# Layer 1 of a graph network on one core: one float32 product a block in place of a float16 and a float32r product

## The chip, the cores and the metric

One program runs on one core of a Trainium2 chip. The metric is the device time of one execution in microseconds (us). A core has a matrix engine (TensorE, PE in the profile; its weight loads are listed apart as PEld), a vector engine (VectorE, DVE), an activation engine (ScalarE, ACT), a general engine (GpSimd, POOL) that issues the indirect transfers, and SyncE (SP) that issues plain ones. SBUF is the on-chip memory of 128 partitions, PSUM the memory that products accumulate in.

## The reference

A layer norm and a relu, then four layers of a graph network over 6250 nodes and 100000 edges, which are sorted by their destination. What the layers compute, cut down:

```python
h = jnp.maximum(_layernorm(x, axis=-1), 0.0)                        # 6250 x 256
deg = segment_sum(ones, dst)
h = h @ W1_self + (segment_sum(h[src], dst) / clip(deg, 1)) @ W1_neigh + b1     # 256 -> 512
hp = relu(h @ W2_pool + b2_pool)
h = h @ W2_self + where(deg > 0, segment_max(hp[src], dst), 0) @ W2_neigh + b2
h = ((segment_sum(h[src], dst) + h) / (deg + 1)) @ W3_neigh + b3
h = h @ W4_self + (segment_sum(h[src], dst) / clip(deg, 1)) @ W4_neigh + b4
out = x + h @ W_fc + b_fc                                           # 6250 x 256
```

The change is in the first `segment_sum(h[src], dst)` and in the rows `h` that it sums.

## The kernel before, in words

The nodes are 49 tiles of 128 (`NT` = 49). Weight matrices that follow one another without a nonlinearity are multiplied together beforehand (`product`). The edges that end in the first tiles are many, since the destinations crowd at low numbers. So layer 1 forms its neighbour sums in two ways.

- **Dense tiles**, the first 12 (`H1`). For each of them a matrix `A` of edge counts (128 x 128 for each of the 49 source tiles, 8-bit) is built by products of one-hot matrices (`build`, `build_narrow`; tile `pb`). Then `dense` multiplies the 49 blocks of `A` with the 49 tiles of rows of `h` and accumulates in the PSUM tile `pd`: 12 x 49 = 588 blocks. A copy of `A` widened to 32 bits (`af`, made by ScalarE) is the stationary operand of the second product.
- **Gathered tiles**, the other 37. `sums` goes through 402 groups of 128 edges. For each, GpSimd gathers the 128 source rows from the table `tab_h` in HBM into a slot of `ring` (13 slots), VectorE writes a one-hot matrix `hot` of the destinations, and PE sums the rows into `pg`. After every four groups VectorE adds `pg` to the accumulators `acc` of the tiles concerned.

`sums` leads: behind each group it calls `hub.advance`, which lays a share of the waiting dense and build products behind it, and steps finished tiles (`done1`) on. A finished tile is divided by its degree, transposed, and multiplied with `Wa` and `Wb`; `turn_h0` transposes the tile's own rows. A scheduler may then move instructions within an engine. In the prologue VectorE's order is fixed by hand.

The rows of `h` are held twice: `Z1h` is the row times 2^20 rounded to float32r, `Z1l` is what the rounding left, as float16. Three more columns of `Z1l` hold 1, the tile's number and the partition's number, so that the same sums also give the degree and a node's sum of source indices. The prologue makes them in 17 groups of three tiles: `stats` and `inverse` (VectorE) find mean and deviation, `scaled` (ScalarE) writes the relu of the normalised row over `xt` and a scaled copy into `Z1h`, `lower` (VectorE) subtracts to get `Z1l` and stores both parts into `tab_h` (386 words a row). Beside this, the prologue sorts out the edges: `row_begins` multiplies one-hot matrices `sel` (float32) with starts `SN` (4 blocks with one product each and 4 blocks with four, 20 in all, into `pa`), and the builds of the first dense tile begin.

So each block takes two products into the same PSUM tile, first the float16 one with 256 + 3 columns, then the float32r one with 256. In `dense`:

```python
nc.tensor.matmul(hold[0][:, : F + extra], a[1], z[1][:, : F + extra], ...)   # L601: float16, 8-bit A
nc.tensor.matmul(hold[0][:, :F], a[0], z[0], ...)                            # L606: float32r, af
```

and in `sums` the same on lines 545 and 548. Products in plain float32 also occur: the weight products (L285), `done1`'s with `Wa` (L1197) and `Wb` (L1203; two for each of 49 tiles), and `row_begins`' (L855). Transposes through PE are products with an identity (`ident`); the ones of `done1`'s means are on L1185.

Layers 2 to 4 follow with tables of their own, and have their own dense and gathered parts that use `sums` and `dense` in other forms.

Of the kernel before, what the change touches and what calls it, by code (L numbers as in the profile page):

```python
# [21 lines left out]
P = 128  # L22
# [7 lines left out]
WIN, WIN2 = 8, 4  # L30
HUB = (12, 23, 23)
WIDE_BUILT = 8
UP = float(2 ** 20)
UP3 = float(2 ** 12)
ROOM3, SEEN3 = float(2 ** 28), float(2 ** 11)
EARLY = (8, 40)
# [52 lines left out]
def fast_path(  # L89
# [81 lines left out]
    const = ctx.enter_context(tc.tile_pool(name="fconst", bufs=1))  # L171
    dram = ctx.enter_context(tc.tile_pool(name="fdram", bufs=1, space=DRAM))

    tab_h = dram.tile([NP, FI + FI // 2 + 2], F32, name="tab_h")
    tab_t = dram.tile([NT, P, FH], F32, name="tab_t")
    tab_r = dram.tile([NP, FH + FH // 2], F32, name="tab_r")
    tab_s = dram.tile([NP, 2 * FO], F32, name="tab_s")
# [323 lines left out]
        return tc.issue_after(ins[0].ins) if ins else nullcontext()  # L501

    def sums(pool, psg, table, F, srcT, keyT, jb, h, done, deep, hub, wait=0, counts=0, todo=None, rest=0,
             wide=False, aside=(), open_accs=3, spare_hots=4):

        ring = pool.tile([P, deep, table.shape[1]], F32R, name="ring", bufs=1)
# [12 lines left out]
        def gather(j):  # L524
            nc.gpsimd.indirect_dma_start(  # L525
                out=ring[:, j % deep, :].bitcast(F32),
                out_offset=None, in_=table,
                in_offset=bass.IndirectOffsetOnAxis(ap=srcT[:, j - jb : j - jb + 1], axis=0),
            )

        for j in range(j0, j0 + ahead):
            one_hot(j)
        for g in range(g_of[h][0], NG):
            pg = bank(psg, "pg", "pg", (2 * F if wide else F + counts,))
            n = min(G, T - g * G)
            for k in range(n):
                j = g * G + k
                X = ring[:, j % deep, :]
                gather(j)
                if j + ahead < T:  # L540
                    one_hot(j + ahead)
                if wide:
                    nc.tensor.matmul(pg, hot[j], X, start=(k == 0), stop=(k == n - 1))  # L543
                else:
                    nc.tensor.matmul(pg[:, : F + counts], hot[j].bitcast(BF16)[:, 1::2],  # L545
                                     X.bitcast(F16)[:, 2 * F : 3 * F + counts],
                                     start=(k == 0), stop=False)
                    mm = nc.tensor.matmul(pg[:, :F], hot[j], X[:, :F], start=False,  # L548
                                          stop=(k == n - 1))
                if counts and j == T - 1:  # L550
                    ended.append(mm)
                del hot[j]
                at = j - j0 + 1
                if at > wait:
                    hub.advance(before + math.ceil((len(hub.work) - before) * (at - wait)
                                                   / (T - j0 - wait - rest)))
                while len(pair) < 2 and todo:
                    pair.append([todo.pop(0), 0])
                for i, t in enumerate(list(pair)):
                    if i and pair[0] is not t and pair[0][1] < 5:  # L560
                        break
                    t[1] += 1
                    if next(t[0], None) is None:
                        pair.remove(t)
                if aside and next(aside[0], None) is None:
                    aside.pop(0)
            for d in range(h, NT):
                g0, g1 = g_of[d]
                if not g0 <= g <= g1:
                    continue  # L570
                m = M[:, m_at[d] + g - g0 : m_at[d] + g - g0 + 1]
                for half in (pg[:, :F], pg[:, F:]) if wide else (pg,):
                    if d not in acc:
                        acc[d] = pool.tile([P, F + counts], F32, name="acc", bufs=open_accs)
                        nc.vector.tensor_scalar(acc[d], half, m, None, op0=ALU.mult)
                    else:
                        nc.vector.scalar_tensor_tensor(acc[d], half, m, acc[d],  # L577
                                                       op0=ALU.mult, op1=ALU.add)
                if g == g1:
                    todo.append(done(d, acc.pop(d)))  # L580
        while aside:
            for _ in aside.pop(0):
                pass
        for t in [t for t, _ in pair] + list(todo):
            for _ in t:
                pass
        del todo[:]

    def dense(ss, block, rows, F, psd, done, extra=0, wide=False, own=None):

        hold = {}

        def run(s):
# [3 lines left out]
            z = rows(s)  # L597
            if wide:
                nc.tensor.matmul(hold[0], a[0], z, start=(s == ss[0]), stop=(s == ss[-1]))  # L599
            else:  # L600
                nc.tensor.matmul(hold[0][:, : F + extra], a[1], z[1][:, : F + extra],  # L601
                                 start=(s == ss[0]), stop=False)
# [33 lines left out]
    def segments():  # L636
# [15 lines left out]
        for b, tb in enumerate(BLOCKS):  # L652
# [20 lines left out]
    nc.gpsimd.memset(Z1l[:, :, FI:], 1.0)  # L673
    nc.gpsimd.iota(Z1l[:, :, FI + 1], pattern=[[1, NT]], base=0, channel_multiplier=0,
                   allow_small_or_imprecise_dtypes=True)
    nc.gpsimd.iota(Z1l[:, :, FI + 2], pattern=[[0, NT]], base=0, channel_multiplier=1,
                   allow_small_or_imprecise_dtypes=True)
    w1pool = layer1.enter_context(tc.tile_pool(name="w1", bufs=1))
    Wa = w1pool.tile([P, KI, FH], F32, name="Wa")
# [18 lines left out]
    with ExitStack() as pro:  # L698
# [59 lines left out]
        def scaled(g):  # L758
# [8 lines left out]
            nc.scalar.activation(Z1h[:, i0 : i0 + LG, :], xt, AF.Copy, scale=UP)  # L767

        def lower(g):
            i0, LG = groups[g]  # L770
            rows = tab_h[i0 * P : (i0 + LG) * P, :]
            hi, lo = Z1h[:, i0 : i0 + LG, :], Z1l[:, i0 : i0 + LG, :]
            nc.vector.scalar_tensor_tensor(lo[:, :, :FI], xts[g], UP, hi.bitcast(F32),
                                           op0=ALU.mult, op1=ALU.subtract)
            nc.sync.dma_start(rows[:, :FI].rearrange("(c p) f -> p c f", p=P), hi.bitcast(F32))
            nc.sync.dma_start(rows[:, FI:].rearrange("(c p) f -> p c f", p=P), lo.bitcast(F32))


        win_of = ep.tile([P, RB * P], F16, name="win_of")
# [254 lines left out]
                rN, dflat[1 : EX + 1].rearrange("(c p e) -> p c e", p=P, e=P)))  # L1034

        def products1():
            yield from product(ep, pst, psm, W1_self, w2p, Wa, 1, 1.0 / UP)
            yield from product(ep, pst, psm, W1_neigh, w2p, Wb, 1, 1.0 / UP)
            yield from bias_rows(psm, b1c, w2p, crow, b2p)

        steps = products1()
# [83 lines left out]
    with ExitStack() as on:  # L1125
# [4 lines left out]
        wk = on.enter_context(tc.tile_pool(name="fl1", bufs=2))  # L1130

        def h0_row(s):
            return Z1h[:, s, :], Z1l[:, s, :]

        def turn_h0(pt, d):
            for k in range(KI):
                c = slice(k * P, (k + 1) * P)
                nc.tensor.matmul(pt[:, k, :], Z1h[:, d, c], ident_r, start=True, stop=False)
# [85 lines left out]
        def widened(i):  # L1224
            if i < len(pieces):
                d, s0 = pieces[i]
                wide[i] = wk.tile([P, LG, P], F32R, name="af", bufs=3)
                nc.scalar.copy(wide[i], As[d % 2][:, s0 : s0 + LG, :])

        def block1(d, s):  # L1230
# [3 lines left out]
            if s % LG == (4 if s >= NT - LG else 0):  # L1234
# [1 line left out]
            return wide[i][:, s % LG, :], As[d % 2][:, s, :]  # L1236

        denses = [dense(range(NT), lambda s, d=d: block1(d, s), h0_row, FI, psd,
                        lambda acc, d=d: todo.append(done1(d, acc)), extra=3)
                  for d in range(H1)]  # L1240
# [7 lines left out]
        sums(wk, psg, tab_h, FI, srcT, keyT, JC * P, H1, done1, 13, hub, counts=3, todo=todo, rest=24, spare_hots=3,  # L1248
             aside=[own_ahead(), tail_checks(wk), segments()])
    layer1.close()  # L1250

# [121 lines left out]
    with tc.tile_pool(name="fl2c", bufs=1) as ck, ExitStack() as late:  # L1373
# [38 lines left out]
        def products2(wp):  # L1412
# [18 lines left out]
            yield from prod(W1_self, us, usA, 1.0 / UP)  # L1431
            yield from prod(W1_neigh, us, usB, 1.0 / UP)
# [382 lines left out]

    upto2.close()

    def stream(pool, chunks, wide_pool, deep=4, ahead=2):

        got = {}  # L1820
        where = {(d, s): i for i, (d, s0, s1) in enumerate(chunks) for s in range(s0, s1)}
# [12 lines left out]
        def widened(i):  # L1834
            if i < len(chunks):
                n = chunks[i][2] - chunks[i][1]
                wide[i] = wide_pool.tile([P, most_wide, P], F32R, name="af", bufs=ahead + 2)
                nc.scalar.copy(wide[i][:, :n, :], got[i][:, :n, :])  # L1838

        for i in range(deep):  # L1840
# [783 lines left out]
```

## Time and profile before

| | |
|---|---|
| median of 3 runs | 2554.43 us (2551.59 to 2556.82) |
| profiled execution | 2551.33 us |
| its span on the core | 2549.5 us |
| mean granted TensorE clock | 0.936 |
| moved by transfers | 781.10 MB |

The profile is of one execution. Its page gives each engine's busy time, strips of 40 equal slices of the span, the transfer queues, the chain of work that ended last, and groups of instructions. A group's row reads: line, engine, operation, what it writes and reads by the program's names (out<-in), shapes, count | busy us, mean ns of one | idle time of the engine just before them and what ended it. The times of overlapping products each include the time in which a result drains, so a group's mean is more than what a product takes from the next one. In the timeline a row is start, length, engine, line and operation, with a count where equal ones are merged. A wait reads: engine, what waited <- what it waited for: us in total, times, longest.

### The profile page before, as it was taken

Reading aid. Unit: us, or ns where it says so; the run is one execution under the profiler, and the core shown is the slowest. Engines: PE = TensorE matmul, PEld = TensorE weight load, DVE = VectorE, ACT = ScalarE, POOL = GpSimd, SP = SyncE. Lnnn points to the kernel's source line nnn. Section 1 sums busy time; section 2 is a strip of 40 time slices with the busy share of each in tenths; the row PEclk is TensorE's granted clock in tenths of the full one; section 3 lists DMA queues with packets and bytes.
Section 4 is the critical chain, followed back from the end, with each engine's and each line's share of the span. In section 5 each row is a group of like instructions: output and inputs, shape, how many; then the busy total and the mean of one; then the engine's idle time right before and its main releaser. Section 6 shows DMA issues by size and latency. Waiting matters only on the chain.

```text
span 2549.5 us, 35257 instructions
## 1 busy us (share of the span) xinstructions
PE 2171.2 (85%) x9379; PEld 1259.7 (49%) x9379; DVE 2044.3 (80%) x5490; ACT 1289.6 (51%) x2685; POOL 1732.9 (68%) x2018
## 2 busy tenths in 40 slices
PE   4789999999687565679999999896399999799987
PEld 2346666767443222234444444342144444488766
DVE  7899998876599899888989999788657778377656
ACT  5679988566378887765323333231112222354443
POOL 5466776667476776777667666677477777477775
PEclk9899999999898787899999999898699999899999
DMA  9667777678799999999999999999799999899996
GB/s 313 177 191 212 215 214 216 203 218 240 248 382 321 332 362 346 335 365 357 342 319 338 343 330 304 302 358 317 255 376 401 402 406 392 292 341 342 324 308 212
DMA packets 380302, 781.10 MB, mean 306 GB/s; under 512 B 56718, under 2 KB 176118, under 8 KB 380060
## 3 DMA queue, kind: packets, MB, share of 16 engines
q0 software_dynamic: 134800, 470.32, 55.4%
q1 hardware_dynamic: 155816, 216.23, 23.5%
q10 hardware_dynamic: 89476, 92.21, 10.9%
q8 instruction: 76, 1.25, 0.2%
q14 instruction: 134, 1.10, 0.1%
HBM read 569.93 MB, written 209.41 MB: 306 GB/s over the span
## 4 chain that ended last, share of the span: by engine, by line
PE 49%; DMA 26%; DVE 13%; issue 4%; ACT 4%; POOL 3%; ACTq 0%; SPq 0%; DVEq 0%; POOLq 0%
PE pd L606 8%; PE pd L601 8%; DMA X<-rows,srcIf 8%; PE pd L599 6%; DMA ring<-tab_r,srcE 6%; PE pm_prf L1620 4%; PE pm_hp L1203 3%; DVE run L1709 3%; PE pm_w L285 2%; PE pm_hp L1197 2%; DMA rows<-X 2%; PE pm_prf L1614 2%; PE pg L545 2%; PE pg L548 2%; PE pm_prf L1617 2%
## 5 line engine op out<-in xcount | busy, mean ns | idle before, releaser
L1728 POOL DMA_INDIRECT X<-rows,srcIf x782 | 743.2, 950 | 315.9 <-issue 143.2
L1709 DVE SCALAR_TENSOR_TENSOR run<-run,samef,X 128x512 f32<-128x512 f32 x758 | 572.9, 756 | 37.3 <-DMA X<-rows,srcIf 32.5
L525 POOL DMA_INDIRECT ring<-tab_h,srcT x402 | 390.8, 972 | 175.4 <-issue 49.6
L1838 ACT CAST af<-ac 128x640 fp32r<-128x640 fp8e4 (+2 forms) x299 | 216.3, 735 | 370.9 <-PE pd L606 143.8
L577 DVE SCALAR_TENSOR_TENSOR acc<-pg,M,acc 128x256 f32<-128x256 f32 (+2 forms) x556 | 282.8, 533 | 52.5 <-PE pg L548 41.7
L525 POOL DMA_INDIRECT ring<-tab_r,srcE x254 | 257.3, 1013 | 94.5 <-issue 33.0
L525 POOL DMA_INDIRECT ring<-tab_s,srcE x254 | 243.9, 960 | 105.1 <-PE pg L543 37.8
L1709 DVE SCALAR_TENSOR_TENSOR X<-X,samef,run 128x512 f32<-128x512 f32 x379 | 281.8, 744 | 34.0 <-issue 12.1
L548 PE MATMUL pg<-ring,hot 128*128 128x256 f32 (+1 forms) x656 | 292.3, 455 | 0.0
L606 PE MATMUL pd<-kept_rows,aw 128*128 128x512 f32 x529 | 271.0, 588 | 0.1
L1664 ACT CAST aw<-ae 128x512 fp32r<-128x512 fp8e4 x184 | 113.8, 620 | 255.8 <-PE pd L606 236.0
L545 PE MATMUL pg<-ring,hot 128*128 128x259 f16 (+1 forms) x656 | 209.4, 322 | 38.8 <-DMA ring<-tab_r,srcE 17.6
L601 PE MATMUL pd<-kept_rows,ae 128*128 128x512 f16 x529 | 209.2, 395 | 9.5 <-DMA ae<-tab_a 6.9
L521 DVE TENSOR_SCALAR hot<-iota_bf,keyE 128x128 fp32r<-128x128 bf16 x508 | 137.7, 298 | 79.6 <-PE pg L543 40.2
L1620 PE MATMUL pm_prf<-unf,hTf 128*128 128x512 f32 x384 | 191.3, 622 | 5.4 <-ACT hTf L1610 4.7
L606 PE MATMUL pd<-Z1h,af 128*128 128x256 f32 x588 | 195.5, 366 | 0.1
L599 PE MATMUL pd<-zt,af 128*128 128x512 f32 x598 | 165.0, 396 | 6.7 <-ACT af L1838 6.7
L548 PEld LDWEIGHTS pg<-ring,hot 128*128 128x128 f32 x656 | 129.0, 197 | 84.0 <-issue 68.5
L601 PEld LDWEIGHTS <-ae 128*128 128x128 fp8e4 x736 | 71.5, 97 | 191.8 <-issue 177.9
L601 PE MATMUL pd<-Z1l,A 128*128 128x259 f16 x588 | 159.8, 282 | 0.2 <-ACT A L379 0.2
L374 PE MATMUL pb<-hm,hs 128*128 128x392 bf16 x461 | 146.7, 344 | 13.2 <-DVE hm L368 11.4
L599 PE MATMUL pd<-z,af 128*128 128x512 f32 x529 | 145.8, 404 | 13.1 <-ACT af L1838 13.1
(415 smaller groups left out, 5028.2 us busy)
## 6 DMA issues: line engine op xcount, KB each, us to landing
rows<-X SPq DMA_DIRECT2D x385, 256.0 KB
rows<-hpf SPq DMA_DIRECT2D x49, 256.0 KB
th<-tab_t ACTq DMA_DIRECT2D x49, 256.0 KB
X<-rows,srcIf POOLq DMA_INDIRECT x782
ae<-tab_a SPq DMA_DIRECT2D x184, 64.0 KB
tab_a<-A ACTq DMA_DIRECT2D x15, 784.0 KB
ac<-tab_a ACTq DMA_DIRECT2D x138, 80.0 KB
tab_t<-th SPq DMA_DIRECT2D x37, 256.0 KB
```

Source lines behind the costliest of these rows:

```text
L374: nc.tensor.matmul(hold[0], hots[0], hots[1], start=(k == 0), stop=(k == k_of[w] - 1))
L525: nc.gpsimd.indirect_dma_start(out=ring[:, j % deep, :].bitcast(F32), out_offset=None, in_=table, in_offset=bass.IndirectOffsetOnAxis(ap=s ...
L545: nc.tensor.matmul(pg[:, : F + counts], hot[j].bitcast(BF16)[:, 1::2], X.bitcast(F16)[:, 2 * F : 3 * F + counts], start=(k == 0), stop=False)
L548: mm = nc.tensor.matmul(pg[:, :F], hot[j], X[:, :F], start=False, stop=(k == n - 1))
L577: nc.vector.scalar_tensor_tensor(acc[d], half, m, acc[d], op0=ALU.mult, op1=ALU.add)
L599: nc.tensor.matmul(hold[0], a[0], z, start=(s == ss[0]), stop=(s == ss[-1]))
L601: nc.tensor.matmul(hold[0][:, : F + extra], a[1], z[1][:, : F + extra], start=(s == ss[0]), stop=False)
L606: nc.tensor.matmul(hold[0][:, :F], a[0], z[0], start=False, stop=(s == ss[-1]))
L1620: nc.tensor.matmul(pm, hT[:, c, :], un[:, c, :], start=False, stop=(c == KH - 1))
L1709: nc.vector.scalar_tensor_tensor(put, held, st, row, op0=ALU.mult, op1=ALU.max)
L1728: nc.gpsimd.indirect_dma_start(out=X[:, k, :], out_offset=None, in_=tab_p, in_offset=bass.IndirectOffsetOnAxis(ap=srcI[:, t : t + 1], axis=0),
L1838: nc.scalar.copy(wide[i][:, :n, :], got[i][:, :n, :])
```

## The change

The rows of `h` are held once, as plain float32 (`Z1`) with the three counting columns behind them, and each block takes one plain float32 product of 259 columns. `scaled` writes its relu straight into `Z1`; `lower` only stores, one transfer of 260 words a row. `hot` and `af` of layer 1 are plain float32 in place of float32r. `turn_h0` is one transpose a half instead of two products. The scale 2^20 and its inverse in the weight products go. The diff, cut to its core:

```diff
-    tab_h = dram.tile([NP, FI + FI // 2 + 2], F32, name="tab_h")
+    tab_h = dram.tile([NP, FI + 4], F32, name="tab_h")
...
+        form = F32 if plain else F32R
+        ring = pool.tile([P, deep, table.shape[1]], form, name="ring", bufs=1)
...
-            hot[j] = pool.tile([P, P], F32R, name="hot", bufs=ahead + spare_hots)
+            hot[j] = pool.tile([P, P], form, name="hot", bufs=ahead + spare_hots)
...
+                elif plain:
+                    mm = nc.tensor.matmul(pg, hot[j], X[:, : F + counts], start=(k == 0),
+                                          stop=(k == n - 1))
                 else:
                     nc.tensor.matmul(pg[:, : F + counts], hot[j].bitcast(BF16)[:, 1::2],
...
+            elif plain:
+                if s == own:
+                    nc.tensor.matmul(hold[0], ident, z, start=(s == ss[0]), stop=False)
+                nc.tensor.matmul(hold[0], a[0], z[:, : F + extra],
+                                 start=(s == ss[0] and s != own), stop=(s == ss[-1]))
...
-    Z1h = zpool.tile([P, NT, FI], F32R, name="Z1h")
-    Z1l = zpool.tile([P, NT, FI + 4], F16, name="Z1l")
+    Z1 = zpool.tile([P, NT, FI + 4], F32, name="Z1")
...
-                nc.scalar.activation(xt[:, c, :], xt[:, c, :], AF.Relu,
+                nc.scalar.activation(Z1[:, i0 + c, :FI], xt[:, c, :], AF.Relu,
                                      bias=nb[:, c : c + 1], scale=rs[:, c : c + 1])
-            nc.scalar.activation(Z1h[:, i0 : i0 + LG, :], xt, AF.Copy, scale=UP)
...
-            hi, lo = Z1h[:, i0 : i0 + LG, :], Z1l[:, i0 : i0 + LG, :]
-            nc.vector.scalar_tensor_tensor(lo[:, :, :FI], xts[g], UP, hi.bitcast(F32),
-                                           op0=ALU.mult, op1=ALU.subtract)
-            nc.sync.dma_start(rows[:, :FI].rearrange("(c p) f -> p c f", p=P), hi.bitcast(F32))
-            nc.sync.dma_start(rows[:, FI:].rearrange("(c p) f -> p c f", p=P), lo.bitcast(F32))
+            nc.sync.dma_start(rows.rearrange("(c p) f -> p c f", p=P), Z1[:, i0 : i0 + LG, :])
...
-                nc.tensor.matmul(pt[:, k, :], Z1h[:, d, c], ident_r, start=True, stop=False)
-                nc.tensor.matmul(pt[:, k, :], Z1l[:, d, c], ident_b, start=False, stop=True)
+                nc.tensor.transpose(pt[:, k, :], Z1[:, d, c], ident)
...
-                wide[i] = wk.tile([P, LG, P], F32R, name="af", bufs=3)
+                wide[i] = wk.tile([P, LG, P], F32, name="af", bufs=3)
```

What stands in PE's row in the middle of layer 1, around the 127th group of `sums`, before the change (a dense block, a gathered group, a build product; `hs` and `A` are stationary operands of their own load):

```order
L601 LDWEIGHTS A_167
L601 MATMUL pd<-Z1l,A_167 128x259
L606 MATMUL pd<-Z1h,af 128x256
L545 LDWEIGHTS hot
L545 MATMUL pg<-ring,hot 128x259
L548 MATMUL pg<-ring,hot 128x256
L374 LDWEIGHTS hs_4341
L374 MATMUL pb<-hm,hs_4341 128x392
```

The same place after it (lines differ by a few; `Z_144` is `Z1`):

```order
L606 MATMUL pd<-Z_144,af 128x259
L545 MATMUL pg<-ring,hot 128x259
L373 LDWEIGHTS hs_4011
L373 MATMUL pb<-hm,hs_4011 128x392
L606 MATMUL pd<-Z_144,af 128x259
```

The order of blocks, groups and builds stays; each pair has become one product, whose weight load the program does not list apart. At the end of layer 1 all 588 blocks stand ahead of the 380th of the 402 groups, where before some 40 of them stood behind the 380th.

VectorE's row in the prologue, at the end of one group's `stats`, before the change:

```order
L746 BN_AGGR mv<-st 128x2
L748 TENSOR_SCALAR sd<-mv 128x3
L773 SCALAR_TENSOR_TENSOR Z1l<-xt,Z1h 128x3x256
L862 COPY atF<-pa 128x8
L863 CAST atI<-atF 128x4
```

And after it:

```order
L753 BN_AGGR mv<-st 128x2
L755 TENSOR_SCALAR sd<-mv 128x3
L864 COPY atF<-pa 128x8
L865 CAST atI<-atF 128x4
L844 TENSOR_SCALAR A_166,within<-A_166,SN 128x782
```

The subtraction is gone from each of the 17 groups, and what stood behind it moves up; nothing is put in its place.

More of the change, by code (lines that the diff above doesn't have):

```diff
@@ L503, in sums @@
     def sums(pool, psg, table, F, srcT, keyT, jb, h, done, deep, hub, wait=0, counts=0, todo=None, rest=0,
-             wide=False, aside=(), open_accs=3, spare_hots=4):
-        ring = pool.tile([P, deep, table.shape[1]], F32R, name="ring", bufs=1)
+             wide=False, plain=False, aside=(), open_accs=3, spare_hots=4):
+        form = F32 if plain else F32R
+        ring = pool.tile([P, deep, table.shape[1]], form, name="ring", bufs=1)
         acc = {}
@@ L525, in gather @@
             nc.gpsimd.indirect_dma_start(
-                out=ring[:, j % deep, :].bitcast(F32),
+                out=ring[:, j % deep, :] if plain else ring[:, j % deep, :].bitcast(F32),
                 out_offset=None, in_=table,
@@ L587, in sums, with dense @@
         del todo[:]
-    def dense(ss, block, rows, F, psd, done, extra=0, wide=False, own=None):
+    def dense(ss, block, rows, F, psd, done, extra=0, wide=False, plain=False, own=None):
         hold = {}
@@ L1036, in products1 @@
         def products1():
-            yield from product(ep, pst, psm, W1_self, w2p, Wa, 1, 1.0 / UP)
-            yield from product(ep, pst, psm, W1_neigh, w2p, Wb, 1, 1.0 / UP)
+            yield from product(ep, pst, psm, W1_self, w2p, Wa, 1)
+            yield from product(ep, pst, psm, W1_neigh, w2p, Wb, 1)
             yield from bias_rows(psm, b1c, w2p, crow, b2p)
@@ L1132, in h0_row @@
         def h0_row(s):
-            return Z1h[:, s, :], Z1l[:, s, :]
+            return Z1[:, s, :]
         def turn_h0(pt, d):
@@ L1238, in fast_path @@
         denses = [dense(range(NT), lambda s, d=d: block1(d, s), h0_row, FI, psd,
-                        lambda acc, d=d: todo.append(done1(d, acc)), extra=3)
+                        lambda acc, d=d: todo.append(done1(d, acc)), extra=3, plain=True)
                   for d in range(H1)]
@@ L1247, in fast_path @@
         hub = Hub(made.rest() + work)
-        sums(wk, psg, tab_h, FI, srcT, keyT, JC * P, H1, done1, 13, hub, counts=3, todo=todo, rest=24, spare_hots=3,
+        sums(wk, psg, tab_h, FI, srcT, keyT, JC * P, H1, done1, 13, hub, counts=3, todo=todo, rest=24, spare_hots=3, plain=True,
              aside=[own_ahead(), tail_checks(wk), segments()])
@@ L1816, in fast_path, with stream @@
     upto2.close()
-    def stream(pool, chunks, wide_pool, deep=4, ahead=2):
+    def stream(pool, chunks, wide_pool, deep=4, ahead=2, form=F32R):
         got = {}
@@ L1836, in widened @@
                 n = chunks[i][2] - chunks[i][1]
-                wide[i] = wide_pool.tile([P, most_wide, P], F32R, name="af", bufs=ahead + 2)
+                wide[i] = wide_pool.tile([P, most_wide, P], form, name="af", bufs=ahead + 2)
                 nc.scalar.copy(wide[i][:, :n, :], got[i][:, :n, :])
```

11 lines of the change are left out of this document (5 added, 6 removed).

## The prediction

> **What bounds the kernel now.** I read first the page: the busy line and the strip of 40 slices (each 63.7 us; a digit is the busy share in tenths, PEclk the granted TensorE clock).
>
> ```profile
> span 2549.5 us, 35257 instructions
> PE 2171.2 (85%) x9379; PEld 1259.7 (49%) x9379; DVE 2044.3 (80%) x5490; ACT 1289.6 (51%) x2685; POOL 1732.9 (68%) x2018
> PE   4789999999687565679999999896399999799987
> DVE  7899998876599899888989999788657778377656
> PEclk9899999999898787899999999898699999899999
> ```
>
> 85% for TensorE (PE) is an average over stages. The change touches the first 660 us only, so the second view is busy time by stretch. The cuts follow the first gather of `tab_h` (95), the point where the dense products set in (180), the narrow builds (500) and the last product of layer 1 (660).
>
> ```profile
> 0.00:40.00 40.00, 9.34 (x35) 6.84 (x36) 26.78 (x102) 16.57 (x34) 20.27 (x244) 1.00 0.97 300
> 40.00:95.00 55.00, 38.00 (x131) 19.82 (x130) 51.64 (x185) 40.60 (x107) 18.43 (x20) 0.80 0.77 237
> 95.00:180.00 85.00, 68.64 (x307) 36.11 (x307) 78.14 (x336) 61.22 (x173) 59.94 (x60) 0.93 0.68 193
> 180.00:500.00 320.00, 318.46 (x1955) 215.88 (x1954) 289.01 (x1119) 274.67 (x642) 221.10 (x227) 1.00 0.71 211
> 500.00:660.00 160.00, 152.12 (x960) 107.88 (x958) 107.95 (x500) 98.81 (x170) 109.50 (x115) 0.98 0.77 232
> 660.00:2549.50 1889.50, 1584.65 (x5997) 873.13 (x5997) 1490.77 (x3252) 797.71 (x1564) 1303.63 (x1353) 0.92 0.96 336
> ```
>
> The columns after the length are PE, PEld, DVE, ACT, POOL busy, then clock, DMA share, GB/s. From 180 to 500 PE is busy 318.46 of 320.00 us at clock 1.00: PE bounds layer 1. Before that VectorE (DVE) bounds: 51.64 of 55.00 in the prologue, 78.14 of 85.00 after it. Whatever PE work is added from 180 to 660 has 1.5 + 7.9 us of idle time to go into, and no more.
>
> **The price of one product.** A busy row's mean contains drain time that the next product overlaps, so I price by start-to-start distance in the timeline. First, a stretch of layer 1 with nothing but dense pairs, and one product that is plain float32 already (L1197, two of 512 columns):
>
> ```profile
> 628.12 0.28 PE L601 MATMUL pd<-Z1l,A 128*128 128x259 f16 x1
> 628.16 0.36 PE L606 MATMUL pd<-Z1h,af 128*128 128x256 f32 x1
> 628.36 0.28 PE L601 MATMUL pd<-Z1l,A 128*128 128x259 f16 x1
> 628.61 0.28 PE L601 MATMUL pd<-Z1l,A 128*128 128x259 f16 x1
> 303.46 1.88 PE L1197 MATMUL pm_hp<-Wa,th 128*128 128x512 f32 x4
> 305.18 0.27 PE L545 MATMUL pg<-ring,hot 128*128 128x259 f16 x1
> 692.57 1.99 PE L285 MATMUL pm_w<-weights,wT 128*128 128x256 f32 x8 [1.01 <-ACT wT L282]
> L1203 PE MATMUL pm_hp<-Wb,th 128*128 128x512 f32 x196 | 93.2, 595 | 0.4 <-DVE hpf L1206 0.4
> L855 PE MATMUL pa<-SN,sel 128*128 128x2 f32 x40 | 7.1, 279 | 7.8 <-DVE SN L844 7.8
> ```
>
> A pair of today, float16 plus float32r, takes 628.61 - 628.12 over two = 0.245 us. L1203 is issued 49 x 2 = 98 times and has 196 records: a plain float32 product runs as two records. L1197's four take 305.18 - 303.46 = 1.72 us, 0.43 each for 512 columns, so 259 columns cost 0.43 x 259/512 = 0.2175 and a whole product 0.435 us. The upper bound is L285, 256 columns: eight in at most 1.99 us, 0.25 each, 0.50 a product; that stretch holds a slow first product and the last one's drain, so I take 0.435. Each pair that becomes a plain product costs PE 0.435 - 0.245 = 0.19 us more.
>
> Two weight loads per product stand beside this:
>
> ```profile
> 303.89 0.19 PEld L1197 LDWEIGHTS pm_hp<-Wa,th 128*128 128x128 f32 x1 [0.24 <-issue]
> 304.32 0.19 PEld L1197 LDWEIGHTS pm_hp<-Wa,th 128*128 128x128 f32 x1 [0.24 <-issue]
> ```
>
> Such a load takes 0.19 us and runs while the record before it streams (0.43 here; 0.2175 in the new product). It fits, with 0.03 us to spare, and costs nothing. If that cover fails, it is the second rival. The Trainium skill (TensorE: Matmul & The Clock Gate, Part 3, The mechanism) says that a weight load overlaps a running product only when it goes to another row group. By that rule these full-height loads would stand bare, two per product. The rows above disagree: the records follow at 0.43 us with loads of 0.19 inside.
>
> **The change, part by part.** The counts and the places with room:
>
> ```profile
> L606 PE MATMUL pd<-Z1h,af 128*128 128x256 f32 x588 | 195.5, 366 | 0.1
> L548 PE MATMUL pg<-ring,hot 128*128 128x256 f32 x402 | 142.7, 370 | 0.0
> L548 PE MATMUL pg<-ring,hot 128*128 128x256 f32 x47 | 17.5, 397 | 0.0
> L606 PE MATMUL pd<-Z1h,af 128*128 128x256 f32 x3 | 1.1, 365 | 0.0
> PE pb L374 <- DVE hm L368: 5.3, 17, 0.6
> PE pg L545 <- DMA ring<-tab_h,srcT: 6.8, 10, 1.3
> L525 POOL DMA_INDIRECT ring<-tab_h,srcT x402 | 390.8, 972 | 175.4 <-issue 49.6 <-PE pb L374 40.8 <-PE pg L548 39.9
> ```
>
> The first two rows are the whole run, the next two the stretch 95 to 180; the first wait is of that stretch, the second of 500 to 660.
>
> 1. Products: 588 dense + 402 sums = 990, times 0.19 = +188 us of PE time.
> 2. Of these, 47 + 3 = 50 fall into 95 to 180, where DVE bounds (PE waits for its `hm`). 50 x 0.19 = 9.5 us goes into PE's 16.4 us of idle time there: -9.5. If none hides, 0; the most is the 16.4.
> 3. From 500 to 660 PE idles 160 - 152.12 = 7.9 us, 6.8 of it for gathered rows. POOL issues a gather in 0.97 us plus its gaps, near what PE eats there; when PE takes 0.19 longer per product the rows are in time. The clock is 0.98 there, 2% of 160 = 3.2 us lost to a half-speed spell after such waits. Both go: -11, or 0 if the waits return.
> 4. `turn_h0`: two products per half, now one transpose:
>
> ```profile
> 629.57 0.22 PE L1138 MATMUL pt_m<-ident_r,Z1h 128*128 128x128 f32 x1
> 629.89 1.08 PE L1203 MATMUL pm_hp<-Wb,th 128*128 128x512 f32 x2
> 631.66 0.38 PE L1185 MATMUL pt_m<-identf,m 128*128 128x128 f32 x2
> 631.88 0.28 PE L601 MATMUL pd<-Z1l,A 128*128 128x259 f16 x1
> ```
>
> The four of today take 629.89 - 629.57 = 0.32 us a tile, two plain transposes 631.88 - 631.66 = 0.22. 49 x 0.10 = -5.
> 5. Prologue: DVE loses the subtraction, ScalarE (ACT) the scaled copy, SyncE (SP) one of two stores per group:
>
> ```profile
> L773 DVE SCALAR_TENSOR_TENSOR Z1l<-xt,Z1h 128x768 f16<-128x768 f32 x11 | 10.5, 951 | 0.0
> L767 ACT ACTIVATE Z1h<-xt 128x768 fp32r<-128x768 f32 x16 | 13.5, 845 | 0.2 <-ACT sd L749 0.2
> 36.45 0.18 DVE L755 RECIPROCAL rs<-sd 128x3 f32<-128x3 f32 x1 [8.08 <-ACT sd L749]
> ```
>
> The 11 big subtractions from 40 to 95 lie on DVE where it is busy 51.64 of 55.00: 10.5 us come off, -10. Of the others four lie ahead of DVE's wait of 8.08 us at 36.45, which would only grow, so I count them as 0; if that wait shrinks as well, 17 x 0.95 = 16 in all. ACT (40.60 of 55.00) and SP are not late there, so 13.5 us of copies and 17 stores bring nothing of their own.
> 6. Rows of 260 instead of 386 words: the gathers move a third less. After item 3 nothing waits for them: 0. `hot` and `af` become float32 in place of float32r, same 4 bytes; ACT and DVE have room from 180 on (274.67 and 289.01 of 320.00, and the stretch gets longer): 0. The change adds no wait. Longer products make DVE's `acc` (behind `pg`) and ACT's `af` (behind `pd`) come later, but those engines then wait for the bound.
> 7. After 660 the program is the same and starts later.
>
> Sum: 188 - 9.5 - 11 - 5 - 10 = +152.5. The profiled execution took 2551.33 us (span 2549.5), so the same execution would take 2704; it lies 3.1 below the median of 2554.43, against which I give 2554.4 + 152.5 = **2707 us**.
>
> **The rivals.**
> - *More of it is hidden.* All idle time of PE from 95 to 660 (16.4 + 1.5 + 7.9), the slow clock (3.2), 16 of the prologue and 5 of the transposes are got: 188 - 50 = +138, 2692. For it: DVE's and ACT's order around PE moves too. Against: waits of one engine for another seldom all vanish. It is inside the range. 0.15.
> - *The first weight load shows.* The first load of a product must fit beside what precedes it, and the narrow build's product streams for less than 0.19. If 0.09 us show on each of the 990 (today's float32r record lasts 0.37 against 0.28 of the float16 one, which points to such a wait), +89: +241, 2796. Against: L1197's records keep 0.43. 0.08.
> - *Both loads stand bare.* 990 x 2 x 0.19 = +376 on top of the forecast: 3083. The L1197 rows speak plainly against it: 0.01. This is what the rule of the Trainium skill quoted above (TensorE: Matmul & The Clock Gate, Part 3, The mechanism) would do here.
> - *Faster.* The stationary operands are zeros, ones and small counts, so the second record might not be needed. One record of 0.2175 in place of 0.245 is 990 x 0.0275 = -27, with -5 and -10: 2512. It decides at 0.245 + 15/990 = 0.26 us a product; above that the change loses. Against it: L855 has one-hot weights too (`sel`), is issued 20 times and has 40 records. 0.02.
> - The rest, 0.02: half for no change, half for a new stall of the order of 100 us.
>
> **How the numbers follow.** Forecast 0.72, more hidden 0.15, first load 0.08, both loads 0.01, faster 0.02, rest 0.02. Own bounds of the forecast: low 188 - 16 - 11 - 5 - 16 = +140 (2694); high, a product at 0.45 (between 0.435 and 0.50, near the lower) and nothing hidden, 990 x 0.205 = +203 (2757). I give 2680 to 2752: a little under the second case's 2692 for a pair that costs more than 0.245 elsewhere today, and short of the high end, since nothing hidden at all is unlikely. This leaves out both load cases, the fast one and the rest, 0.13, and the tails. A measurement of this kernel tells about 0.2% (5 us) from no change. Faster 0.02, same 0.01, slower 0.97.
>
> **What would show it.** In the profile after: 1176 records into layer 1's `pd` and 804 into its `pg`, all of 259 columns, the two of a product 0.22 us apart; PE full from 180 on at clock 1.00 and layer 1's last product near 660 + 152 = 812; the first gather near 85; no wait for `ring<-tab_h` at the end of layer 1; 1889 us from there to the end, as now. Starts of 0.31 within a product mean bare loads, 588 records into `pd` the fast rival. If layer 1 ends before 780 or after 860, a term of the sum is wrong.

## The result, and the profile after

The changed kernel takes 2700.7 us (median of 6 runs, 2697.79 to 2711.84), the kernel before 2554.02 us in the same rounds (6 runs, 2548.0 to 2558.25): a ratio of 1.0591, 95% interval 1.0569 to 1.0613. The prediction was 2707 us, 2680 to 2752, slower with a chance of 0.97. The profiled execution took 2699.74 us, with a span of 2697.8.

The page of the changed kernel, its busy line and strips (a slice is now 67.4 us):

```profile
span 2697.8 us, 35042 instructions
PE 2347.6 (87%) x9281; PEld 1401.6 (52%) x9281; DVE 2060.8 (76%) x5473; ACT 1292.6 (48%) x2668; POOL 1726.0 (64%) x2018
PE   5799999999997947657898999989559999899998
DVE  6996876665647998988887999979846777557656
```

PE's run of nines has grown from seven slices to ten, and VectorE's digits under it, 6 to 9 before, are 4 to 8 from the fourth slice on: over most of layer 1 PE alone is full. Busy time by stretch (length, then PE, PEld, DVE, ACT, POOL, the granted clock, DMA share, GB/s), with the cuts of before and one more at the new end of layer 1, 815:

```profile
40.00:95.00 55.00, 41.06 (x138) 20.93 (x136) 46.35 (x211) 35.29 (x103) 21.64 (x24) 0.78 0.60 195
95.00:180.00 85.00, 75.49 (x314) 42.60 (x314) 80.82 (x323) 65.37 (x181) 58.96 (x60) 1.00 0.53 151
180.00:500.00 320.00, 320.00 (x1411) 229.16 (x1410) 235.09 (x851) 228.46 (x528) 165.79 (x174) 1.00 0.42 124
500.00:660.00 160.00, 160.00 (x704) 114.61 (x703) 96.22 (x376) 76.19 (x140) 76.59 (x81) 1.00 0.41 122
660.00:815.00 155.00, 155.00 (x691) 115.89 (x690) 83.41 (x356) 76.00 (x126) 79.43 (x84) 1.00 0.49 148
815.00:2697.80 1882.80, 1584.35 (x5991) 870.53 (x5989) 1493.41 (x3252) 797.34 (x1562) 1304.04 (x1353) 0.92 0.96 337
```

From 180 to 815 PE is busy the whole 635 us, at clock 1.00 throughout: the 1.5 and 7.9 us of idle time and the 0.98 of before are gone. Behind that the last row is the last row of before (1882.80 against 1889.50 us long, PE 1584.35 against 1584.65 busy), moved.

The groups of the changed products, their weight loads and the gathers, and then three steps of the timeline near the end of layer 1:

```profile
L606 PE MATMUL pd<-Z,af 128*128 128x259 f32 x1176 | 332.2, 384 | 0.0
L545 PE MATMUL pg<-ring,hot 128*128 128x259 f32 x804 | 238.9, 385 | 5.4 <-DVE acc L580 1.9 <-DMA ring<-tab_h,srcT 1.3 <-DVE hs L359 0.7
L606 PEld LDWEIGHTS pd<-Z,af 128*128 128x128 f32 x1176 | 212.5, 190 | 51.3 <-issue 1.2
L525 POOL DMA_INDIRECT ring<-tab_h,srcT x402 | 386.3, 961 | 338.9 <-PE pg L545 168.3
787.18 0.60 PE L545 MATMUL pg<-ring,hot 128*128 128x259 f32 x2
787.62 1.47 PE L606 MATMUL pd<-Z,af 128*128 128x259 f32 x6
788.93 0.60 PE L545 MATMUL pg<-ring,hot 128*128 128x259 f32 x2
798.73 0.38 PE L1140 MATMUL pt_m<-identf,Z 128*128 128x128 f32 x2
798.95 0.38 PE L1186 MATMUL pt_m<-identf,m 128*128 128x128 f32 x2
```

588 blocks have 1176 records and 402 groups have 804, so a product is two. Six records take 788.93 - 787.62 = 1.31 us, 0.218 each, so a product takes 0.437 us where the pair took 0.245. `turn_h0`'s two transposes take 798.95 - 798.73 = 0.22 a tile where four took 0.32. The gathers wait more, and most of it for PE: behind the products into `pg` they stand 168.3 us (last figure of L525), against 39.9 before.

Where the stages lie, before (first three rows) and after (last three): the first product into `pd` (each row counts those of a short stretch and gives the first and last start), the last sum of layer 1 in the timeline, and the first gather of layer 2.

```profile
L601 PE MATMUL pd<-Z1l,A x20: 273/275/285, 178.3 to 198.4; 128*128 128x259 f16 x20
662.29 0.36 PE L548 MATMUL pg<-ring,hot 128*128 128x256 f32 x1
L1728 POOL DMA_INDIRECT X<-rows,srcIf x127: 940/946/1437, 677.7 to 849.9; - x127
```

```profile
L606 PE MATMUL pd<-Z,af x46: 382/382/382, 168.6 to 199.7; 128*128 128x259 f32 x46
813.77 1.04 PE L545 MATMUL pg<-ring,hot 128*128 128x259 f32 x4
L1729 POOL DMA_INDIRECT X<-rows,srcIf x17: 942/946/974, 828.3 to 849.0; - x17
```

The dense products set in 9.7 us earlier; from there to the end of the last sum (662.65 and 814.81) it takes 646.2 us instead of 484.3, +161.9; from that to layer 2's first gather 13.5 instead of 15.1 (-1.6), and from there to the end 1869.5 instead of 1871.8. Together -9.7 + 161.9 - 1.6 - 2.3 = +148.3 us of span.

### The profile page after: what moved, and what is told of

The parts are those of the page before. It is cut to its first block, busy times and chain, and to the rows that moved or that the text cites. A ratio compares the mean times of both kernels' runs of the same rounds, so it can differ in the third digit from the quotient of the medians.

```text
span 2697.8 us, 35042 instructions
## 1 busy us (share of the span) xinstructions
PE 2347.6 (87%) x9281; PEld 1401.6 (52%) x9281; DVE 2060.8 (76%) x5473; ACT 1292.6 (48%) x2668; POOL 1726.0 (64%) x2018
## 5 line engine op out<-in xcount | busy, mean ns | idle before, releaser
L525 POOL DMA_INDIRECT ring<-tab_h,srcT x402 | 386.3, 961 | 338.9 <-PE pg L545 168.3
L606 PE MATMUL pd<-Z,af 128*128 128x259 f32 x1176 | 332.2, 384 | 0.0
L525 POOL DMA_INDIRECT ring<-tab_r,srcE x254 | 258.5, 1018 | 92.2 <-issue 34.1
L525 POOL DMA_INDIRECT ring<-tab_s,srcE x254 | 245.0, 964 | 103.4 <-PE pg L543 30.1
L545 PE MATMUL pg<-ring,hot 128*128 128x259 f32 x804 | 238.9, 385 | 5.4 <-DVE acc L580 1.9
L606 PEld LDWEIGHTS pd<-Z,af 128*128 128x128 f32 x1176 | 212.5, 190 | 51.3 <-issue 1.2
L545 PEld LDWEIGHTS pg<-ring,hot 128*128 128x128 f32 x804 | 143.2, 190 | 67.0 <-issue 34.2
L521 DVE TENSOR_SCALAR hot<-iota_bf,keyT 128x128 f32<-128x128 bf16 x402 | 114.4, 290 | 81.5 <-PE pg L545 79.5
L432 ACT ACTIVATE A<-pb 128x392 fp8e4<-128x392 f32 x240 | 116.6, 495 | 86.6 <-PE pb L426 86.3
```

The lines of the kernel that those rows point to most:

```text
L525: nc.gpsimd.indirect_dma_start(out=ring[:, j % deep, :] if plain else ring[:, j % deep, :].bitcast(F32), out_offset=None, in_=table, in_of ...
L545: mm = nc.tensor.matmul(pg, hot[j], X[:, : F + counts], start=(k == 0), stop=(k == n - 1))
L606: nc.tensor.matmul(hold[0], a[0], z[:, : F + extra], start=(s == ss[0] and s != own), stop=(s == ss[-1]))
```

## The experiments

The theory is the prediction's: a plain float32 product is two full-length records, PE bounds layer 1, and the prologue gives 10 us back through VectorE. `split`, `one_r`, `prologue_back` and `halves16` ran together on a chip on which the kernel before took 2958.09 us, for a reason that stays open; of them only ratios to that and distances within a trace are used. All but `split` ran once more on another chip, where the kernel before took 2552.47.

**The changed kernel again.** No edit.

> The changed kernel itself, unaltered, as the reference for the others of this call, since the earlier call's kernels ran where the kernel before took 2958 us. If the machine is as in the first measurement: 2700 us and 1.059 times the kernel before. If transfers and code loading are as slow as in the earlier call: near 3025 us, and a smaller ratio, since the part of layer 1 that PE does not bound is then longer in the kernel before.

2701.73 us (2696.98 to 2712.18) against 2552.47, ratio 1.0601 (1.0576 to 1.0627). The first gather starts at 88.2 us, the dense products at 169.5: within 1 us of the first execution of the changed kernel. Together the two measurements give 1.0596.

**Shorter records under the same weight loads.** Each dense product, except the first of a tile, is cut into two over 128 and 131 columns, so that each block has four weight loads and four records of half the length:

```diff
-                nc.tensor.matmul(hold[0], a[0], z[:, : F + extra], ...)
+                    for c0, c1 in ((0, P), (P, F + extra)):
+                        nc.tensor.matmul(hold[0][:, c0:c1], a[0], z[:, c0:c1], ...)
```

> The changed kernel with each dense product (all but a tile's first block) cut into two products of 128 and 131 columns: four records of about 0.109 us in place of two of 0.218, and four weight loads in place of two, for 576 blocks. If weight loads are hidden whatever the record's length: the same 0.437 us a block, 2700 us. If a load holds the next record up for its whole 0.19 us: 4 x 0.19 = 0.76 us a block, 576 x 0.32 = +186, 2887 us. If only part of a load holds it up (a float32r record started 0.03 us late behind a float16 one of 0.108 before the change): 4 x 0.14 = 0.56, +70, 2770 us. My theory that the cover is there with little to spare says between 2770 and 2887.

3015.41 us, ratio 1.0205 (1.0146 to 1.0264) to its own kernel before. The changed kernel did not run on that chip, so this time says nothing on the loads; the trace does. One block in its timeline, and what follows it; the second row is the block's weight loads:

```profile
300.34 0.61 PE L610 MATMUL pd<-Z,af 128*128 128x128 f32 x4
300.17 0.58 PEld L610 LDWEIGHTS pd<-Z,af 128*128 128x128 f32 x4
300.78 0.38 PE L1144 MATMUL pt_m<-identf,Z 128*128 128x128 f32 x2
```

Four records take 300.78 - 300.34 = 0.44 us, no more than the two that they replace. The cover of the weight loads was not thin at all: a load is listed with 0.19 us, but four of them start within 0.58 - 0.19 = 0.39 us, so they also overlap each other, and records of half of 0.218 us hide them. I had expected that little is to spare here; that was wrong. The rivals that price the loads are gone with it, as they are by the 0.437 us of the changed kernel itself.

**One record instead of two.** Rows, `hot` and `af` become float32r in place of float32, 260 columns (the edit, cut to its core):

```diff
-        form = F32 if plain else F32R
+        form = F32R
-    Z1 = zpool.tile([P, NT, FI + 4], F32, name="Z1")
+    Z1 = zpool.tile([P, NT, FI + 4], F32R, name="Z1")
-                wide[i] = wk.tile([P, LG, P], F32, name="af", bufs=3)
+                wide[i] = wk.tile([P, LG, P], F32R, name="af", bufs=3)
```

It leaves out what the rounding to float32r takes from the rows.

> The changed kernel with layer 1's rows, one-hot matrices and widened counts as float32r, so that a block takes one record of 260 columns; it leaves out what rounding the rows to float32r takes away. Table, transfers, prologue and order stay those of the changed kernel. If the second record is the price (my theory): PE needs 0.14 to 0.2 us a block instead of 0.437, it no longer bounds layer 1, and the gathers (402 at 1.25 us) or VectorE do: layer 1 ends at 610 to 650 us instead of 815, 2490 to 2540 us in all. If the price lay in the wider table row, the loads or the prologue, it stays near 2700.

> As the earlier one_r (one float32r record of 260 columns a block; leaves out what rounding the rows takes away), beside the changed kernel. A block's record was 0.115 to 0.12 us there, so PE loses 990 x 0.32 = 317 us of work; gathers at 1.25 us each (503 in all) and VectorE remain: layer 1 ends at 610 to 650 us and the whole takes 2490 to 2540 us where the changed one takes 2700. If the second record were not the price, 2700.

First run 2931.1 us, ratio 0.9886 (0.9849 to 0.9924); second 2519.39 against 2552.47, ratio 0.9882 (0.9862 to 0.9903), the last sum ends at 625.4 us. In the second, one dense record and what follows it, the same stretch as above, and PE's two largest waits from 180 to 625:

```profile
306.54 0.28 PE L606 MATMUL pd<-Z,af 128*128 128x260 f32 x1
306.66 0.34 PE L373 MATMUL pb<-hm,hs 128*128 128x392 bf16 x1
180.00:500.00 320.00, 286.65 (x1380) 183.86 (x1379) 298.25 (x1204) 284.27 (x661) 240.25 (x247) 0.94 0.60 178
PE pg L545 <- DMA ring<-tab_h,srcT: 21.4, 23, 2.0
PE pb L373 <- ACT A L378: 16.3, 17, 1.6
```

A block is now one record, here of 306.66 - 306.54 = 0.12 us (some take 0.15), in place of two of 0.218. The whole loss turns into a gain of 1.2%, and PE is no longer full: it waits for gathered rows and for ScalarE. So the price lies in the float32 product, since the table, the transfers and the order are those of the changed kernel. This run takes away the second record and nearly halves the first, so it does not tell the number of the records from their length.

**Two float16 parts.** The kernel before, with the row held as a float16 and a float16 of what is left (516 columns with the counts), both multiplied with `A` and `hot` as they are, without the widened copy. It leaves out the lowest bits that two float16 parts don't hold.

```diff
-    Z1h = zpool.tile([P, NT, FI], F32R, name="Z1h")
-    Z1l = zpool.tile([P, NT, FI + 4], F16, name="Z1l")
+    Z1 = zpool.tile([P, NT, 2 * FI + 4], F16, name="Z1")
+                nc.tensor.matmul(hold[0], a, z[:, : F + extra], ...)
+                nc.tensor.matmul(hold[0][:, :F], a, z[:, F + 4 :], ...)
```

> A version of the kernel before: the row is held as float16 plus its rounding rest as float16 (2 x 256 columns and the counting ones, 258 words a table row), both products take the 8-bit or bfloat16 stationary operand, no widened copy, no scale. A float32r record and its float32 load of 0.2 us become a float16 one with a load of 0.1. If the load is what makes a pair 0.245 instead of 2 x 0.108 us: 0.22 to 0.23 a pair, 990 x 0.015 to 0.025 = -15 to -25, 2530 to 2540 us. If gathers or VectorE take over as the bound: about 2550, as before.

> As the earlier halves16 (two float16 rows, 8-bit and bfloat16 stationary operands, no widened copy). Its pair took 0.222 us in the earlier trace against 0.245: 990 x 0.023 = -23 us of PE work against the kernel before; 2530 us where that takes 2554. If gathers bound layer 1 instead: about 2550.

First 2909.6 us, ratio 0.9824 (0.9775 to 0.9873); then 2524.28 against 2552.47, ratio 0.9894 (0.9877 to 0.991). From the second, a piece of the timeline and the same stretch:

```profile
400.56 0.27 PE L606 MATMUL pd<-Z,A 128*128 128x259 f16 x1
400.67 0.27 PE L607 MATMUL pd<-Z,A 128*128 128x256 f16 x1
400.79 0.27 PE L606 MATMUL pd<-Z,A 128*128 128x259 f16 x1
400.90 0.27 PE L607 MATMUL pd<-Z,A 128*128 128x256 f16 x1
180.00:500.00 320.00, 316.62 (x2059) 213.20 (x2057) 288.31 (x1174) 241.95 (x600) 232.27 (x241) 1.00 0.59 173
```

A pair takes 0.11 + 0.11 = 0.22 us, half of the plain product's 0.437 and 0.02 less than today's pair, and PE is still all but full. This version beats both kernels: it is 28 us (1.1%, with an interval clear of no change) faster than the one before and 177 us faster than the changed one.

**The prologue's 10 us, first try.** ScalarE's copy and VectorE's subtraction are put back into the changed kernel on tiles that nothing else reads, the subtraction reading the copy:

```diff
+            nc.scalar.activation(spare_h[:, :LG, :], Z1[:, i0 : i0 + LG, :FI], AF.Copy, scale=1.0)
+            nc.vector.scalar_tensor_tensor(spare_l[:, :LG, :], Z1[...], 1.0, spare_h[...], ...)
```

> The changed kernel with the removed copy (ScalarE) and subtraction (VectorE) put back into the prologue on tiles that nobody reads, 17 of each of the old shapes. If VectorE bounds the prologue as I summed it: the first gather about 7 to 10 us later, 2708 to 2711 us. If the prologue hides them: 2701. If all 17 counted: 2717.

> As the earlier prologue_back (removed ScalarE copy and VectorE subtraction put back on tiles nobody reads), beside the changed kernel on the same chip: 7 to 10 us more than after_again if VectorE bounds the prologue, none if the prologue hides them.

First 3033.4 us, ratio 1.0263 (1.0216 to 1.031); then 2733.27 against 2552.47, ratio 1.0713 (1.0693 to 1.0734): 32 us over the changed kernel, more than three times the 7 to 10 that I had put on it. VectorE's largest wait from 0 to 130 us says why:

```profile
DVE spare_l L781 <- ACT spare_h L774: 26.5, 15, 3.3
```

VectorE stood behind the copy 15 times, and the first gather starts at 115.4 us only. No such wait is among those of the kernel before, though its subtraction reads a copy too. The edit has one spare tile for all groups, and in program order the next group's copy (`scaled(g + 1)`) stands ahead of a group's subtraction (`lower(g)`), so each subtraction reads the copy after its own: the second starts at 21.21 us, when the third copy ends (20.33 + 0.84), where in the kernel before the second subtraction (18.02) is ahead of the third copy (18.61). So this measures my edit and not the change. The next four runs put the parts back without that tie.

**The prologue's parts, each alone.** The subtraction reads a still tile of ones, the copy is read by nothing, and the wide table has rows of 386 words with a second store of 126 words per group:

```diff
# dve_back
+            nc.vector.scalar_tensor_tensor(spare_l[:, :LG, :], Z1[...], 1.0, still[:, :LG, :], ...)
# act_back
+            nc.scalar.activation(spare_h[:, :LG, :], Z1[:, i0 : i0 + LG, :FI], AF.Copy, scale=1.0)
# wide_table
-    tab_h = dram.tile([NP, FI + 4], F32, name="tab_h")
+    tab_h = dram.tile([NP, FI + FI // 2 + 2], F32, name="tab_h")
+            nc.sync.dma_start(rows[:, FI + 4 :]..., Z1[:, i0 : i0 + LG, : FI // 2 - 2])
```

> The changed kernel with only VectorE's subtraction put back in the prologue: 17 operations of 128 x 768 per group of three blocks (one smaller), float16 out, reading Z1 and a still tile of ones, so that it waits for nothing that ScalarE does beyond Z1 itself. My theory (VectorE bounds from 40 to 95 us; 11 of the 17 of 0.95 us each count): first gather near 95 to 98, 7 to 10 us slower than the changed kernel's 2701, so 2708 to 2711. Rival 1 (the subtraction was hidden, the prologue's gain came from ScalarE's copy or the second store): first gather near 88, within 3 us of 2701. Rival 2 (all 17 count): 16 us, 2717.

> The changed kernel with only ScalarE's copy of 128 x 768 per group put back, into a tile that nothing reads. My theory (ScalarE has room, 40.60 of 55.00 us busy from 40 to 95): within 3 us of the changed kernel's 2701, first gather near 88 to 90. Rival (ScalarE's Z1 and its square roots come later, and VectorE's reciprocals wait for them): 16 copies of 0.85 us, up to 13 us slower, first gather near 100.

> The changed kernel with the table's and the ring's rows at 386 words as before: a second store of 126 words per group in the prologue, and gathers that carry a half more; the last 126 words are copies that no product reads. My theory (nothing waits for the gathers in layer 1, and the stores end early): within 4 us of the changed kernel's 2701. Rival (the narrower rows brought part of the 11 us at the end of layer 1): waits of PE for ring<-tab_h of 5 us or more from 500 to 815, and 5 to 10 us slower.

2707.82, 2709.22 and 2710.67 us against 2551.75: ratios 1.0611 (1.0589 to 1.0634), 1.0612 (1.0588 to 1.0635) and 1.0619 (1.0597 to 1.0642). Against 1.0596 that is 4 to 6 us each, and the intervals reach 6 us, so the times alone settle none of the three. The traces, one of each kernel, say more. The first and last start of the gathers up to about 121 us, one fence for each kernel: before, the changed one, then `dve_back`, `act_back`, `wide_table`.

```profile
L525 POOL DMA_INDIRECT ring<-tab_h,srcT x21: 942/946/1796, 94.8 to 120.9; - x21
```

```profile
L525 POOL DMA_INDIRECT ring<-tab_h,srcT x25: 942/946/1632, 88.3 to 120.0; - x25
```

```profile
L525 POOL DMA_INDIRECT ring<-tab_h,srcT x24: 942/947/1680, 90.4 to 120.8; - x24
```

```profile
L525 POOL DMA_INDIRECT ring<-tab_h,srcT x19: 942/946/1607, 96.6 to 120.0; - x19
```

```profile
L525 POOL DMA_INDIRECT ring<-tab_h,srcT x20: 947/949/1746, 94.7 to 119.5; - x20
```

VectorE's subtraction alone moves the first gather by 2.1 us, ScalarE's copy by 8.3, the wider rows with their second store by 6.4 (a second trace of the changed kernel lies 0.1 us from the first). My theory had them at 7 to 10, 0 and 0: wrong in all three. The first dense product goes the same way: 178.3 us before, 168.6 changed, then 170.9, 177.0 and 176.2. The stretch 40 to 95 agrees, first of `dve_back` and then of `wide_table`:

```profile
40.00:95.00 55.00, 37.95 (x133) 19.19 (x131) 53.00 (x215) 33.02 (x96) 21.75 (x23) 0.78 0.58 187
```

```profile
40.00:95.00 55.00, 37.52 (x118) 20.33 (x119) 41.19 (x165) 32.50 (x96) 16.53 (x20) 0.72 0.74 233
```

In `dve_back` VectorE does 6.65 us more in the stretch than in the changed kernel's 46.35, and does it in idle time; in `wide_table` it does 5 us less than there and still the stretch's end comes later.

Ahead of the first gather the same steps stand in all these traces: VectorE's last `mkf`, GpSimd's copy of it, and 3.8 to 4.2 us after that copy's start the gather. Pieces of the chain of work that leads there (start, length, engine, what), of the kernel before and of `act_back`:

```profile
85.81 0.87 DVE Z1l L773
86.68 0.35 DVE sel L925
89.89 0.69 DVE mkf L933
```

```profile
87.31 0.60 ACT Z L774
88.06 0.32 ACT spare_h L776
88.56 0.44 DVE sel L930
91.86 0.69 DVE mkf L938
```

Before the change a subtraction stands right ahead of these steps, so VectorE's own work did hold them up. With the copy alone put back, the copy stands in that place, and VectorE waits 1.3 us for ScalarE. So several chains end close together here, and to shorten one brings the next to light. Which transfer holds `wide_table` up the trace does not say; that stays open.

From 500 to 815 us `wide_table` shows no wait of PE at all, so the narrower rows brought nothing at the end of layer 1, as item 6 of the prediction had it.

**All three parts at once.**

```diff
+ the edits of dve_back, act_back and wide_table together
```

> The changed kernel with all three prologue parts put back at once and independent of each other: VectorE's subtraction, ScalarE's copy, and the second store with rows of 386 words. Alone they moved the first gather from 88.3 to 90.4, 96.6 and 94.7 us. My theory now (three chains that share the prologue; the longest decides, so the parts overlap): first gather at 95 to 98, near the 94.8 of the kernel before, and 2709 to 2713. Rival (each adds to one chain): 2.1 + 8.3 + 6.4 on top of 88.3, first gather near 105, and 2718 or more.

2712.47 us (2707.24 to 2728.92) against 2551.55, ratio 1.0637 (1.0609 to 1.0666). Over the changed kernel's 1.0596 that is 10 us; with the widths of both intervals taken together, 2 to 19. Its first gathers and its stretch 40 to 95:

```profile
L525 POOL DMA_INDIRECT ring<-tab_h,srcT x20: 942/946/1494, 94.7 to 119.7; - x20
40.00:95.00 55.00, 35.64 (x129) 18.39 (x127) 51.21 (x184) 40.80 (x107) 17.85 (x20) 0.81 0.80 241
```

The first gather is back at 94.7 against 94.8 before, and the stretch is that of before (DVE 51.21 against 51.64, ACT 40.80 against 40.60). The first dense product starts at 175.8 us. The parts overlap instead of adding up (they would give 105): ScalarE's copy or the second store alone keeps the prologue as long as it was.

## Why the prediction was right, point by point

The forecast was +152.5 us; the span grew by 148.3, the median by 146.7. The large term and its mechanism were right. The small ones were not all, and that they come out so near is in part luck: the prologue gave 3.5 us less than forecast, and the stretch behind it 3.2 more.

- *What bounds.* Right. PE is full from 180 to 815, and no other engine is busy for over 74% of any stretch there.
- *Item 1, the price.* 0.435 us a product and 0.19 more than a pair; measured 0.437 and 0.192. `one_r` shows that the float32 product is the cause, though not the second record by itself, and the 1176 records rule out the fast rival.
- *The weight loads.* Right that they cost nothing, wrong that 0.03 us was all there was to spare: `split` hides them under records of half the length. By the rule of the Trainium skill (TensorE: Matmul & The Clock Gate, Part 3, The mechanism) that a load overlaps a product only in another row group (the section's text also names a background weight buffer) they would stand bare; in the changed kernel and in `split` these full-height loads run beside the products (two loads listed with 0.19 us each in a product of 0.437), so neither agrees with it. The Trainium skill (FP8 and Floating Point Precision, TensorE Precision Notes) counts four passes through the array for a true float32 product; the runs agree, 0.437 us against 0.11 for a float16 record, though the profile lists them as two records.
- *Item 2, products in the cover of VectorE.* Between 95 and 180 PE got through 97 records of sums (some 48 products) and 22 of dense products (11). That these are hidden was right. More came on top: from the first gather to the first dense product it takes 80.3 us instead of 83.5, which I had at no change. PE's idle time in the stretch went from 16.4 to 9.5 us, and the clock from 0.93 to 1.00, which I had not counted; whether that is the reason no run tells.
- *Items 3 and 4.* From the dense start to the last sum I had 940 products at 0.19 = +178.6, less 11 and 5: +162.6. Measured +161.9. The waits for `ring<-tab_h` at the end are gone, `turn_h0` went from 0.32 to 0.22 a tile.
- *Item 5, the prologue.* Of the 10 us 6.5 came: the first gather starts at 88.3 us, where I had it near 85. The 9.7 at the first dense product hold the 3.2 of item 2 besides. `all_back` gives 6.4 back at the first gather and 7.2 at the first dense product; its time (10 us, 2 to 19) can't tell these apart. The step that failed is that ScalarE's copy and the second store "bring nothing of their own". VectorE's own work did stand last before, but the others were close behind: put back alone, the copy moves the first gather by 8.3 us and the wider rows with their store by 6.4, the subtractions by 2.1. With the copy left in the gather starts at 96.6 us, with the wide rows left in at 94.7, and before the change it started at 94.8. VectorE's 51.64 of 55.00 us is a poor witness in a stretch in which the engines take turns: its wait for ScalarE's square roots grew in the changed kernel from 8.8 to 13.5 us, as the next two rows say (VectorE's waits from 0 to 100, before and after), and with the subtractions back (`dve_back`) it is 5.8.

```profile
DVE rs L755 <- ACT sd L749: 8.8, 2, 8.1
```

```profile
DVE rs L762 <- ACT sd L756: 13.5, 8, 7.0
```

- *Item 7.* The rest was to stay the same and came out 3.9 us shorter (15.1 to 13.5 and 1871.8 to 1869.5). With the terms above nearly cancelling, that is most of the difference between +152.5 and +148.3; executions of one kernel differ by more than that (2548.0 to 2558.25), so I read no cause into it.

## What to carry to other kernels

Price a product by the distance from one start to the next, count its records, and take the price only where the engine is full: here one row of a product that already ran in plain float32 gave the price of the new one to 1%. A float32 row against a matrix that float16 or bfloat16 holds exactly was cheaper here as two float16 products (0.22 us) than as one float32 product (0.437), if the bits that they drop may go. An engine that is nearly always busy in a stretch of short, mutually dependent steps need not be its only bound: put each removed piece back alone, and without a new dependence, before crediting it.

## What the runs showed of the hardware that I had not expected

- Weight loads of 128 x 128 float32, listed with 0.19 us each, start less than that apart: four of them beside four records of 0.11 us cost nothing that shows.
- A float16 record of 256 to 259 columns follows in 0.11 us, so the pair of today (0.245) was itself not at its best: what is left of it for the float32r record is 0.135 us, an estimate by difference, against 0.11 for the float16 one in its place. In `one_r`, where it has no float16 record beside it, a float32r record of 260 columns takes 0.12 to 0.15; no run shows what makes the difference.
